# Self-attention values by token tiles, attention parts fetched three ahead and expert rows four ahead, and the last bias as a product with ones

## The chip, the cores and the metric

The kernel is one program on one core of one Trainium2 chip, written against the engines' own instructions, with a tile framework that allocates buffers and sets semaphores. The metric is the device time of one execution in microseconds (us), of which the median of several runs is taken. The core has TensorE (PE: matmuls and transposes; its weight loads are listed as PEld), VectorE (DVE), ScalarE (ACT), GpSimd (POOL) and SyncE (SP, which issues DMA transfers in order). In this kernel nearly all transfers are issued on SP.

## The reference

One decoder layer over 16 batches of 100 tokens, 512 wide, in float32: causal self attention, cross attention to 361 context tokens with grouped heads, and a mixture of 8 experts of which each token uses two. Every stage ends in a sum with its input and a layer norm.

```python
x = _layernorm(x + _L0_attn_ref(x, w_q, w_k, w_v, w_o))        # 16 heads of 32, causal
x = _layernorm(x + _L0_xattn_ref(x, ctx, mask, ...))           # 16 heads of 128, 4 kv heads, RMS-normed q, k
x = _layernorm(x + _L0_ffn_ref(x, ...))

def _L0_ffn_ref(x, ...):
    logits = x @ router_w + router_b;  topk_w = softmax(top2(logits))
    h = silu(x @ expert_w[e] + expert_b[e])                    # only the chosen two count
    combined = sum_e h_e * topk_w_e
    y = x + (combined @ proj_w + proj_b)
    return norm_w * (y / sqrt(mean(y*y) + 1e-6))
```

## The kernel before

All products are float32 products made from pairs. `split` (L133) makes of a float32 tile a rounded high half (a cast, mostly on ACT, L137) and a low half (a subtraction on DVE or POOL, L140); `mm3` (L143) is three matmuls, high by high, low by high and high by low (L145, L146, L147). In instruction names WH and WL are the halves of a weight or of a shared buffer. A product over 512 is four chunks of 128, so 12 matmuls. Most engines' work is emitted in Python order and then ordered by a scheduler; `in_turn` and `keep_in_program_order` pin single instructions. Each engine runs its own queue in order, and a buffer of a pool is taken anew when the last reader of its old tile is done.

The work is staged as follows.

- A, self attention (0 to about 215 us). Four groups of four batches (400 tokens), four chunks of four heads each: 16 units `heads4`. Extra work (splits, the next group's queries, keys and values, and the loads of stage B) is put between the steps of a unit by a table, `at(unit, step, function)` (L488 to L537). `self_v(g, r)` (L301) makes the values of one batch: 100 tokens as columns of the stationary side, 512 columns moving, 12 matmuls, and one copy from PSUM to the tile `v` by ACT.
- B, output product, residual, layer norm, cross-attention queries (to about 400 us).
- C, cross attention (about 400 to 1073 us). For each of 16 batches and 4 kv heads, one head group: `x_scores` (L736), softmax on DVE, ACT and POOL, transposes `x_turn` (L762), `x_attend` (L771), and the store of the result `o` to DRAM (`od`, L792). The loop L862 to L899 writes out the order by hand, with the next batch's key and value products between. In the last batch there is no next batch, and parts of stage D are put there instead.
- D, output product of cross attention, by parts: a part is one tile of 128 tokens (T of 13) times the four heads of one kv head (g of 4), 48 matmuls into a PSUM bank `acc`. The last three tiles are walked g by g. `d_load(i)` (L817) fetches the part's attention result `of` from DRAM on SP and splits it to `ot_h`, `ot_l`; `d_part(i)` (L826) is its product; `d_norm(t)` (L846) fetches the residual `x1d`, adds, normalises and stores to `x2d`; `d_turn(t)` (L928) transposes the tile for the router, and then adds the last bias, `x2+pb`, on POOL (L941) and stores that to DRAM as `xbd` (L942). `d_logits` (L944) is the router product. Routing (choose, settle and slots, L1058 to L1277) is a long chain of small DVE operations with a few products `gb`. `load_expert(e)` (L1337) loads and splits four rows of an expert's weights at once, at some tiles of the loop L1351 to L1387. In the pool `d_in` there are 2 buffers of `of`; a part is fetched when its predecessor's split has freed a buffer.
- E, expert slots: `e_gather` (L1296) fetches the tokens of a slot from `x2d` by index, then turn, product `ph`, bias `eb`, activation, store.
- F, the end: combine, and the last product. `f_load` loads the bias-carrying residual `z` from `xbd` (L1503 to L1507) and `x2`; `f_product` (L1536) is 12 matmuls into `pp`; `f_square` (L1543) adds `pp` to `z` (L1546) and squares.

## Time and profile before

| | |
|---|---|
| runs (3): median, lowest, highest | 1408.28, 1403.09, 1411.89 us |
| the profiled execution: its time | 1403.04 us |
| its span, first to last instruction | 1401.2 us |
| granted TensorE clock, mean | 0.979 |
| matrix instructions on PE | 7952 |
| DMA over the span | 159.79 MB, mean 114 GB/s |

The profile is one execution. Busy times are shares of its span; the slices divide the span in 40, a digit is the busy share of a slice in tenths. In rows of waits, "A <- B: total, times, longest" says that A's engine waited for B. In a timeline a row is start, duration, engine, line, operation, out<-in, shape, and in brackets the idle time of that engine before it and what ended it. Matmuls overlap: the time that one costs is the distance of its start to the next start, and not its duration.

### The profile page before, as it was taken

What the parts mean: (1) busy time and instruction counts of PE and PEld (TensorE: products, weight loads), DVE (VectorE), ACT (ScalarE), POOL (GpSimd) and SP (SyncE); (2) the same over time, 40 slices, a digit from 0 to 9 for tenths busy, and PEclk for the clock granted to TensorE, in tenths of its full rate; (3) what the DMA queues carried; (4) which work ended last, traced back from release to release, by engine and by line L of the source; (5) the groups of instructions that cost most, each with busy time, mean ns of one, the idle gap of its engine ahead of it and who ended that gap; (6) DMA issues with size and microseconds to landing.
All of it is one profiled execution on the core that took longest, in us unless ns stands there. A gap on an engine that the chain in (4) does not pass through costs nothing. (4 is left out here: it accounts for less than half of the span.)

```text
span 1401.2 us, 25131 instructions
## 1 busy us (share of the span) xinstructions
PE 1334.0 (95%) x7952; PEld 1107.1 (79%) x7952; DVE 938.7 (67%) x2932; ACT 757.9 (54%) x1899; POOL 712.5 (51%) x839
## 2 busy tenths in 40 slices
PE   8999989999999999999999999999999898899995
PEld 7888878888878888888888878888888676687783
DVE  5766576766556777777777666777754557764587
ACT  4666653444445666666666656666654233333356
POOL 6877763344245455555555545555554545532630
PEclk9999999999999999999999999999999999899997
DMA  5231144654452123323333123322435544667874
GB/s 160 73 94 49 58 143 127 141 105 116 90 108 60 50 69 75 72 71 78 77 70 75 46 64 78 77 65 55 108 107 155 197 165 151 188 228 254 271 239 152
DMA packets 197872, 159.79 MB, mean 114 GB/s; under 512 B 133322, under 2 KB 152878, under 8 KB 197742
## 3 DMA queue, kind: packets, MB, share of 16 engines
q1 hardware_dynamic: 187904, 137.83, 35.6%
q0 software_dynamic: 4576, 14.95, 3.5%
q10 hardware_dynamic: 5262, 5.41, 1.3%
q8 instruction: 65, 1.06, 0.3%
q14 instruction: 65, 0.53, 0.1%
HBM read 107.16 MB, written 50.99 MB: 113 GB/s over the span
## 5 line engine op out<-in xcount | busy, mean ns | idle before, releaser
L759 POOL TENSOR_SCALAR p<-p,sums 100x361 f32<-100x361 f32 x256 | 146.5, 577 | 100.0 <-DVE sums L758 89.0
L746 DVE CUSTOM_DVE_ANT_0 p<-s,nmask 100x361 f32<-100x361 f32 x256 | 132.9, 526 | 63.9 <-PE s L147 55.2
L757 ACT ACTIVATE p<-p,nm 100x361 f32<-100x361 f32 x256 | 153.2, 601 | 40.3 <-DVE nm L746 37.0
L140 DVE TENSOR_TENSOR pT_l<-ptp,pT_h 128x400 fp32r<-128x400 f32 (+1 forms) x192 | 107.4, 567 | 56.2 <-ACT pT_h L137 55.5
L145 PE MATMUL pq<-WH 128*128 128x512 f32 (+2 forms) x272 | 106.7, 392 | 6.2 <-DVE WH L139 5.4
L140 POOL TENSOR_TENSOR cT_l<-cf,cT_h 128x512 fp32r<-128x512 f32 (+1 forms) x48 | 54.3, 1133 | 104.6 <-ACT cT_h L137 102.6
L767 PE MATMUL ptp<-ident,p 100*128 100x100 f32 (+1 forms) x768 | 107.2, 251 | 0.0
L137 ACT CAST pT_h<-ptp 128x400 fp32r<-128x400 f32 (+1 forms) x192 | 91.2, 486 | 29.6 <-PE ptp L767 29.2
L767 PEld LDWEIGHTS ptp<-ident,p 100*128 100x128 f32 (+1 forms) x768 | 95.3, 151 | 13.3 <-POOL p L759 2.3
L146 PE MATMUL pq<-WL,WH 128*128 128x512 f32 (+2 forms) x272 | 104.0, 382 | 0.0
L147 PE MATMUL pq<-WH,WL 128*128 128x512 f32 (+2 forms) x272 | 103.8, 381 | 0.0
L147 PE MATMUL acc<-WH,ot_l 128*128 128x512 f32 (+1 forms) x208 | 85.9, 414 | 7.8 <-DVE ot_l L140 6.3
L145 PE MATMUL acc<-WH,ot_h 128*128 128x512 f32 (+1 forms) x208 | 85.5, 411 | 5.7 <-ACT ot_h L137 5.7
L145 PE MATMUL s<-kT_h,WH 128*100 128x362 f32 x256 | 87.7, 353 | 0.7 <-ACT kT_h L137 0.7
L145 PE MATMUL av<-pT_h,WH 128*128 128x400 f32 (+1 forms) x192 | 76.8, 400 | 8.7 <-ACT pT_h L137 8.3
L146 PE MATMUL acc<-WL,ot_h 128*128 128x512 f32 (+1 forms) x208 | 84.3, 405 | 0.0
L147 PE MATMUL s<-kT_h,WL 128*100 128x362 f32 x256 | 84.2, 329 | 0.0
L614 POOL TENSOR_TENSOR qs<-qs,r_q 128x512 f32<-128x512 f32 (+1 forms) x52 | 54.0, 1069 | 59.4 <-DVE r_q L169 49.3
L146 PE MATMUL s<-kT_l,WH 128*100 128x362 f32 x256 | 83.7, 327 | 0.0
L140 POOL TENSOR_TENSOR WL<-qf,WH 128x400 fp32r<-128x400 f32 x64 | 67.3, 1053 | 30.0 <-ACT WH L137 26.2
L145 PE MATMUL pv<-WH,cT_h 128*128 128x512 f32 (+1 forms) x192 | 79.9, 416 | 0.9 <-DVE WL L140 0.9
L146 PE MATMUL pv<-WL,cT_h 128*128 128x512 f32 (+1 forms) x192 | 78.1, 407 | 0.0
(337 smaller groups left out, 4003.5 us busy)
## 6 DMA issues: line engine op xcount, KB each, us to landing
qf<-qd SPq DMA_DIRECT2D x64, 200.0 KB, 2.9
of<-od SPq DMA_DIRECT2D x48, 256.0 KB, 3.6
cf<-in_ctxT SPq DMA_DIRECT2D x16, 722.0 KB, 4.1
eb<-in_expert_b SPq DMA_DIRECT2D x32, 256.0 KB, 4.3
ysd<-h SPq DMA_DIRECT2D x32, 256.0 KB, 4.4
f_e<-in_expert_w SPq DMA_DIRECT2D x30, 256.0 KB, 4.6
f_wq<-in_Wq SPq DMA_DIRECT2D x16, 256.0 KB, 3.3
f_wo<-in_Wo SPq DMA_DIRECT2D x16, 256.0 KB, 4.4
```

The costliest lines, as they stand in the source:

```text
L137: ins = nc.scalar.copy(dst.h, src)
L140: low.tensor_tensor(dst.l, src, dst.h.bitcast(FP), ALU.subtract)
L145: nc.tensor.matmul(out, a.h, b.h, start=start, stop=False)
L146: nc.tensor.matmul(out, a.h, b.l, start=False, stop=False)
L147: nc.tensor.matmul(out, a.l, b.h, start=False, stop=stop)
L614: nc.gpsimd.tensor_tensor(qr[:, hs, :], qr[:, hs, :], rs[:n, hs].unsqueeze(2).to_broadcast([n, GR, HD2]), ALU.mult,)
L746: nc.vector.tensor_tensor_reduce(out=p, in0=sc[:, :SE], in1=nmask, scale=1.0, scalar=BIG, op0=ALU.add, op1=ALU.min, accum_out=nm,)
L757: nc.scalar.activation(p, p, AF.Exp, bias=nm, scale=-1.0, accum_out=sh)
L759: nc.gpsimd.tensor_scalar(p, p, sh, 1.0, ALU.mult, ALU.mult)
L767: nc.tensor.transpose(pt[:n, h, :], probs[h][:, c0 : c0 + n], ident[:S, :S])
```

## The change

Three things change, and some buffers with them.

1. Values of self attention. Group 0 is made by batch as before (`self_v_batch`). For groups 1 to 3, `self_v(g, t)` makes three tiles of 128 tokens, and their rows are moved by SP from SBUF to SBUF into the four batches' tiles. The remaining 16 tokens of each of the three groups (48 in all) come through a new input `xlT` and one product `self_v_last`. Stage B's pools open and its loads start some steps later.
2. Inputs of D. The fetch of a part (`d_fetch`) is parted from its split (`d_load`). The first five parts are fetched into `d_in`, the later ones, three ahead, into the pool `xsp` (4 buffers, tag `xs`), which is also that of the gathered tokens and opens when C has closed. Expert weights are fetched row by row, four rows ahead, and one row is split every two parts, behind the part's own cast. Gathers are emitted at the fourth part from the end. Router weights load earlier.
3. The last bias. `x2+pb`, its 13 stores and 13 loads go. `pb` is split to two rows, 0 and 32, of a 33-row tile, and a matmul with ones adds it to `pp` in PSUM; `f_square` adds `x2` instead of `z`. Small tiles of the end share tags, and `z` has 4 buffers instead of 5.

```diff
@@ -298,15 +301,59 @@
-    def self_v(g, r):
-        pv = bank("mm" if g else "t", [S, D], f"pv_{g}_{r}")
+    def self_v_batch(r):
+        pv = bank("t", [S, D], f"pv_0_{r}")
         mmk(
             pv,
-            lambda k: xg[g][:, k, r * S : (r + 1) * S],
+            lambda k: xg[0][:, k, r * S : (r + 1) * S],
             lambda k: units["wv_s"][:, k, :],
         )
-        V[g, r] = w1.tile([S, D], FP, name=f"v_{g}_{r}", tag="v", bufs=8)
-        nc.scalar.copy(V[g, r], pv)
+        V[0, r] = w1.tile([128, D], FP, name=f"v_0_{r}", tag="v", bufs=8)
+        nc.scalar.copy(V[0, r][:S], pv)
+    NL = (NG - 1) * REST_V
+    def fetch_x_last():
+        XF["l"] = stage.tile([128, D], FP, name="xl_f", tag="f")
+        nc.sync.dma_start(XF["l"][:, : KC * NL], xlT.rearrange("p k n -> p (k n)"))
+    def split_x_last():
+        xg["l"] = slot_of(5)[:, 0, : KC * NL].rearrange("p (k n) -> p k n", n=NL)
+        f = XF["l"][:, : KC * NL].rearrange("p (k n) -> p k n", n=NL)
+        split(xg["l"], f, nc.vector, nc.gpsimd)
+    def self_v_last():
+        pv = bank("mm", [NL, D], "pv_last")
+        mmk(pv, lambda k: xg["l"][:, k, :], lambda k: units["wv_s"][:, k, :])
+        V["l"] = w4.tile([NL, D], FP, name="v_last")
+        nc.scalar.copy(V["l"], pv)
+    def self_v(g, t):
+        pv = bank("mm", [128, D], f"pv_{g}_{t}")
+        mmk(
+            pv,
+            lambda k: xg[g][:, k, t * 128 : (t + 1) * 128],
+            lambda k: units["wv_s"][:, k, :],
+        )
+        for r in range(GB) if t == 0 else ():
+            V[g, r] = w1.tile([128, D], FP, name=f"v_{g}_{r}", tag="v", bufs=8)
+        if t == 0:
+            vt = V[g, 0]
+        else:
+            vt = xp.tile([128, D], FP, name=f"vt_{g}_{t}", tag="f", bufs=2)
+        nc.scalar.copy(vt, pv)
+        a = S if t == 0 else t * 128
+        while a < (t + 1) * 128:
+            r, o = divmod(a, S)
+            m = min(S - o, (t + 1) * 128 - a)
+            nc.sync.dma_start(V[g, r][o : o + m], vt[a - t * 128 : a - t * 128 + m])
+            a += m
+        if t == 2:
+            a = (g - 1) * REST_V
+            nc.sync.dma_start(V[g, GB - 1][S - REST_V : S], V["l"][a : a + REST_V])
...
@@ -474,9 +521,9 @@
-    def fetch_row(name, s, src, k):
+    def fetch_row(name, s, src, k, p=stage):
         units[name] = slot_of(s)
-        f = stage.tile([128, D], FP, name=f"f_{name}_{k}", tag="f")
+        f = p.tile([128, D], FP, name=f"f_{name}_{k}", tag="f")
         tc.keep_in_program_order(nc.sync.dma_start(f, src[:, k]))
@@ -505,9 +552,14 @@
                     at(u, 1, split_x, g + 1, 2 + k)
-            if c > 1:
-                for r in range(2):
-                    at(u, 1 + 2 * r, self_v, g + 1, 2 * (c - 2) + r)
+            if c == 2:
+                at(u, 1, self_v, g + 1, 0)
+                at(u, 3, self_v, g + 1, 1)
+            if c == 3:
+                at(u, 1, self_v, g + 1, 2)
+    at(2, 1, fetch_x_last)
+    at(2, 3, split_x_last)
+    at(3, 0, self_v_last)
@@ -526,12 +578,12 @@
     AHEAD = 5
-    at(10, 0, b_open)
-    for t, i in enumerate((44, 48, 52, 54, 58)):
+    at(12, 0, b_open)
+    for t, i in enumerate((48, 50, 52, 54, 58)):
         at(i // 4, i % 4, b_fetch, t)
-        i += 2 if t == AHEAD - 1 else 4
+        i += 2 if t in (0, AHEAD - 1) else 4
         at(i // 4, i % 4, behind, b_split, t)
-    for t, i in enumerate((51, 55, 59, 61, 62)):
+    for t, i in enumerate((53, 56, 59, 61, 62)):
         at(i // 4, i % 4, b_out, t)
...
@@ -576,6 +628,10 @@
     nc.vector.tensor_scalar(nmask, nmask, -1.0, None, ALU.mult)
+    rw = kvk.tile([128, KC, NE], FP, name="rw")
+    nc.scalar.dma_start(rw, router_w.rearrange("(k p) e -> p k e", p=128))
+    rb = kvk.tile([128, NE], FP, name="rb")
+    nc.scalar.dma_start(rb, router_b.partition_broadcast(128))
     qkw = const.tile([128, 3], FP, name="qkw")
@@ -804,24 +860,33 @@
     order = [(b, g) for b in range(B) for g in range(NKV)]
-    OT, X1 = {}, {}
+    OT, OF, X1 = {}, {}, {}
+    split_last = [None]
         inp["d"] = pool(d_i, "d_in", 2)
+        inp["of"] = inp["d"], "f"
+    def d_fetch(i):
+        t, g = parts[i]
+        n = TT[t][1]
+        p, tag = inp["of"]
+        f = p.tile([128, D], FP, name=f"of_{t}_{g}", tag=tag)
+        OF[i] = f = f.rearrange("p (h n) -> p h n", n=128)[:, :, :n]
+        nc.sync.dma_start(f, od[t][:, g * GR : (g + 1) * GR, :n])
     def d_load(i):
         n = TT[t][1]
-        p = inp["d"]
-        of = p.tile([128, GR, 128], FP, name=f"of_{t}_{g}", tag="of")
-        nc.sync.dma_start(of[:, :, :n], od[t][:, g * GR : (g + 1) * GR, :n])
-        OT[t, g] = pair(p, [128, GR, 128], f"ot_{t}_{g}", tag="ot")
-        split(OT[t, g][:, :, :n], of[:, :, :n], low=nc.vector if i % 2 else nc.gpsimd)
+        OT[t, g] = pair(inp["d"], [128, GR, 128], f"ot_{t}_{g}", tag="ot")
+        split_last[0] = split(
+            OT[t, g][:, :, :n], OF.pop(i), low=nc.vector if i % 2 else nc.gpsimd
+        )
@@ -863,8 +928,10 @@
                 d_open()
+                d_fetch(0)
                 d_load(0)
             for j in range(HEAD * g, HEAD * (g + 1)):
+                d_fetch(j + 1)
                 d_load(j + 1)
@@ -905,6 +972,8 @@
     xsp = pool(fin, "k_x", 4, side="right")
+    inp["of"] = xsp, "xs"
     gs = ExitStack()
@@ -913,14 +982,6 @@
-    rw = gw.tile([128, KC, NE], FP, name="rw")
-    nc.scalar.dma_start(rw, router_w.rearrange("(k p) e -> p k e", p=128))
-    rb = gw.tile([128, NE], FP, name="rb")
-    nc.scalar.dma_start(rb, router_b.partition_broadcast(128))
-    pb = gw.tile([128, D], FP, name="pb")
-    nc.scalar.dma_start(pb, proj_b.partition_broadcast(128))
-    xbd = [dram.tile([128, D], FP, name=f"xbd_{t}") for t in range(NT)]
     lg = gw.tile([128, NT, NE], FP, name="lg")
@@ -938,8 +999,6 @@
         nc.scalar.copy(XT2[t][:, :, :n], pt[:, :, :n])
-        nc.gpsimd.tensor_tensor(x2[:n], x2[:n], pb[:n], ALU.add)
-        nc.sync.dma_start(xbd[t][:n], x2[:n])
@@ -1334,32 +1393,61 @@
-    def load_expert(e, last=False):
+    def load_last(e):
         for k in range(KC):
-            if last and k > 1:
-                f = raw[:, k - 2]
-            else:
-                f = stage.tile([128, D], FP, name=f"f_e_{e}_{k}", tag="f")
-                tc.keep_in_program_order(nc.sync.dma_start(f, kp(expert_w[e])[:, k]))
             split(
                 slot_of(e)[:, k],
-                f,
-                nc.vector if last and k == 1 else nc.scalar,
-                nc.vector if last and k else nc.gpsimd,
-            )
+                raw[:, k - 2] if k > 1 else ROW.pop((f"e_{e}", k)),
+                nc.vector if k == 1 else nc.scalar,
+                nc.vector if k else nc.gpsimd,
+            )
+    BY = (NT - TAIL) * NKV
+    erows = [(e, k) for e in early for k in range(KC)]
+    split_at = [HEAD * NKV + 2 + 2 * r for r in range(len(erows))]
+    assert split_at[-1] < BY + TAIL
+    for g in range(NKV - 1):
+        first = BY + TAIL * (g + 1)
+        erows += [(wo_slot[g], k) for k in range(KC)]
+        split_at += [first + min(k, TAIL - 1) for k in range(KC)]
+    erows += [(wo_slot[-1], k) for k in range(2)]
+    split_at += [len(parts)] * 2
+    rows_in, rows_out = [0], [0]
+    ROWS = 4
+    def e_rows(i):
+        while rows_out[0] < len(erows) and split_at[rows_out[0]] <= i:
+            e, k = erows[rows_out[0]]
+            in_turn(split_row(f"e_{e}", k), split_last[0])
+            rows_out[0] += 1
+            e_fetch()
+    def e_fetch():
+        while rows_in[0] < min(rows_out[0] + ROWS, len(erows)):
+            r = rows_in[0]
+            fetch_row(f"e_{erows[r][0]}", erows[r][0], kp(expert_w[erows[r][0]]),
+                      erows[r][1], inp["d"] if r % 5 > 2 else stage)
+            rows_in[0] += 1
+    begun = HEAD * NKV + 1
+    e_fetch()
     for i in range(HEAD * NKV, len(parts)):
         t, g = parts[i]
+        while begun < min(i + 4, len(parts)):
+            d_fetch(begun)
+            begun += 1
         if i + 1 < len(parts):
             d_load(i + 1)
+        e_rows(i)
         among = {}
                 among = d_logits(t - 1)
-            if g == 0 and t in (2, 4, 6, 8):
-                load_expert(early[t // 2 - 1])
         elif t > NT - TAIL and g == 0:
@@ -1371,8 +1459,6 @@
                 d_norm(t)
-        if t == NT - 1 and g < NKV - 1:
-            load_expert(wo_slot[g])
         if (t, g) == (CUT, 0):
@@ -1382,12 +1468,10 @@
             slots(0, EARLY, CUT)
-        if (t, g) == (NT - 1, 1):
+        if i == len(parts) - 4:
             for k in range(4):
                 e_gather(k)
-    d_i.close()
-    ck_l.close()
-    load_expert(wo_slot[3], True)
+    load_last(wo_slot[3])
     e_turn(0)
@@ -1405,6 +1489,8 @@
     d_l.close()
+    d_i.close()
+    ck_l.close()
     e_l = ExitStack()
@@ -1446,6 +1532,19 @@
+        f = stage.tile([128, D], FP, name="f_pb", tag="f")
+        b = inp["f1"].tile([33, D], FR, name="pb")
+        nc.gpsimd.memset(f[:33], 0.0)
+        for r in (0, 32):
+            nc.scalar.dma_start(f[r : r + 1], proj_b.rearrange("(o n) -> o n", o=1))
+        nc.scalar.copy(b, f[:33])
+        nc.vector.tensor_tensor(
+            b[32:33], f[32:33], b[32:33].bitcast(FP), ALU.subtract
+        )
+        inp["pb"] = b
+        inp["one"] = inp["f1"].tile([33, 128], FR, name="one_r")
+        nc.gpsimd.memset(inp["one"].bitcast(FP), 1.0)
     def f_weights(k):
@@ -1497,14 +1596,14 @@
         else:
-            z = inp["f2"].tile([128, D], FP, name=f"z_{t}", tag="z", bufs=5)
+            z = inp["f2"].tile([128, D], FP, name=f"z_{t}", tag="z", bufs=4)
             x2 = stage.tile([128, D], FP, name=f"x2_{t}", tag="f")
         L[t] = x2, z
-        for dst, src in ((z, xbd[t]), (x2, x2d[t0 : t0 + n])):
-            if not tail:
-                nc.sync.dma_start(dst[:n], src[:n])
-            else:
-                tc.keep_in_program_order(nc.scalar.dma_start(dst[:n], src[:n]))
+        src = x2d[t0 : t0 + n]
+        if not tail:
+            nc.sync.dma_start(x2[:n], src)
+        else:
+            tc.keep_in_program_order(nc.scalar.dma_start(x2[:n], src))
@@ -1537,18 +1636,22 @@
         pp = bank("av", [128, D], f"pp_{t}")
-        mmk(pp[:n], lambda f: cp[:, f, :n], lambda f: inp["pw"][:, f, :])
+        nc.tensor.matmul(
+            pp[:n], inp["one"][:, :n], inp["pb"], start=True, stop=False
+        )
+        for f in range(KC):
+            mm3(pp[:n], cp[:, f, :n], inp["pw"][:, f, :], False, f == KC - 1)
         F[t] = pp
         pp, (x2, y) = F[t], L[t]
-        nc.vector.tensor_tensor(y[:n], pp[:n], y[:n], ALU.add)
-        ss = tiny(1, f"yss_{t}", "yss")
+        nc.vector.tensor_tensor(y[:n], pp[:n], x2[:n], ALU.add)
+        ss = tiny(1, f"yss_{t}", "ln_v")
         nc.scalar.activation(pp[:n], y[:n], AF.Square, accum_out=ss[:n])
         to = C.pop(t) if t >= LATE else y
-        sn = tiny(1, f"yn_{t}", "yn")
+        sn = tiny(1, f"yn_{t}", "rs_y1")
         nc.vector.tensor_tensor_reduce(
...
```

More of the change, by code (lines that the diff above doesn't have):

```diff
@@ L31 @@
 GT = GB * S
+REST_V = GT % 128
 TT = [(t, min(128, T - t)) for t in range(0, T, 128)]
@@ L67, in tile_decoder_layer @@
     xT: bass.AP,
+    xlT: bass.AP,
     ctxT: bass.AP,
@@ L226, in tile_decoder_layer @@
     w3 = pool(a_l, "a_3", 8)
+    w4 = pool(a_l, "a_4", 1)
     ps.append(pool(a_l, "ps_a", 2, space=PSUM))
@@ L406, in self_attend @@
                     av[32 * j : 32 * j + 32, r, :],
-                    V[g, r][:, h : h + 32],
+                    V[g, r][:S, h : h + 32],
                     PT[g, c, j][:, r, :],
@@ L541, in tile_decoder_layer @@
     self_scores(*heads4[0])
-    self_v(0, 0)
+    self_v_batch(0)
     split_chunk(1)
     for r in range(1, GB):
-        self_v(0, r)
+        self_v_batch(r)
     self_q(0, 1)
@@ L1607, in f_first @@
         if t < REST:
-            s = tiny(1, f"s_{t}", "f_s")
+            s = tiny(1, f"s_{t}", "rs_a1")
             nc.vector.tensor_tensor(s, v, r, ALU.mult)
@@ L1612, in f_first @@
         nc.vector.scalar_tensor_tensor(y[:n], x2[:n], s[:n], y[:n], ALU.mult, ALU.add)
-        nm = tiny(1, f"nm3_{t}", "ln_nm")
+        nm = tiny(1, f"nm3_{t}", "rs_t1")
         nc.vector.tensor_scalar(nm[:n], F[t][1][:n], -(D**-1.5), None, ALU.mult)
-        var = tiny(1, f"var_{t}", "ln_var")
+        var = tiny(1, f"var_{t}", "rs_r1")
         nc.scalar.activation(
@@ L1791 @@
         "xT": x.reshape(NG, GT, KC, 128).transpose(0, 3, 2, 1),
+        "xlT": x.reshape(NG, GT, KC, 128)[1:, GT - REST_V :]
+        .transpose(3, 2, 0, 1)
+        .reshape(128, KC, (NG - 1) * REST_V),
         "ctxT": np.asarray(ctx_2048).reshape(B, SE, KC, 128).transpose(0, 3, 2, 1),
```

## The prediction

> **What bounds the kernel now.** I read the page's busy shares first, then its forty slices, then what TensorE (PE) waits for after 1050 us.
>
> ```profile
> span 1401.2 us, 25131 instructions
> PE 1334.0 (95%) x7952; PEld 1107.1 (79%) x7952; DVE 938.7 (67%) x2932; ACT 757.9 (54%) x1899; POOL 712.5 (51%) x839
> ...
> PE   8999989999999999999999999999999898899995
> ```
>
> PE is busy 95% of the span, so work taken off PE where its slices show 9 counts in full, and work taken off another engine counts only where PE waits for it. The dips are the first slice, slices 31 to 34 (the parts of the Wo product, stage D) and the end. The waits of PE from 1050 us on (us in total, times, longest) say who is late there:
>
> ```profile
> PE acc L147 <- DVE ot_l L140: 6.0, 5, 2.7
> PE acc L145 <- ACT ot_h L137: 5.7, 2, 2.9
> PE ptc L1526 <- DVE y L1517: 4.0, 2, 2.9
> ...
> PE acc L147 <- POOL ot_l L140: 1.5, 1, 1.5
> ```
>
> 13.5 us of D (6.0 + 5.7 + 1.5 and small ones, with 1.2 for `ptx` 14.7) go to halves of an attention part that are late. Who makes them late is in the waits of SP's queue, 1050 to 1250:
>
> ```profile
> SPq L851 <- DMA xbd<-x: 17.9, 8, 3.8
> SPq L822 <- POOL ot_l L140: 16.0, 10, 2.7
> SPq L942 <- POOL x L941: 11.6, 10, 2.6
> ```
>
> SP issues in order: the fetch of a part (L822) and the residual (L851) stand behind stores of `x2+pb`. One stall in the timeline, with ACT casting in order too:
>
> ```profile
> 1176.77 0.62 ACT L137 CAST WH<-f_e 128x512 fp32r<-128x512 f32 x1 [4.17 <-DMA f_e<-in_expert_w]
> 1177.30 0.40 ACT L137 CAST ot_h<-of 128x256 fp32r<-128x256 f32 x1
> ...
> 1177.75 0.45 PE L145 MATMUL acc<-WH,ot_h 128*64 128x512 f32 x1 [2.92 <-ACT ot_h L137]
> ...
> 1178.50 0.63 PE L145 MATMUL acc<-WH,ot_h 128*128 128x512 f32 x1
> 1178.93 0.63 PE L146 MATMUL acc<-WL,ot_h 128*128 128x512 f32 x1
> ```
>
> ACT sat 4.17 us on an expert row with the part's cast behind it. The matmuls after the gap start .43 us apart instead of .233: eight of them cost 8 × (.427 − .233) = 1.6 us more. That follows three gaps (near 1110, 1178 and 1192 us): 4.8 us on top.
>
> **The change part by part.** The sum goes against the profiled execution, 1403.04 us with a span of 1401.2. The three runs' median, 1408.28, lies 5.2 above it.
>
> *1. Self values by token tiles.* Groups 1 to 3 had 4 batches × 12 matmuls, 144; now 3 tiles × 3 × 12 = 108, and 12 for all the last rows (48): −24. The stream is 512 columns either way, and the trace has them .233 apart:
>
> ```profile
> 63.85 0.40 PE L145 MATMUL pv<-WH 128*100 128x512 f32 x1
> 64.08 0.39 PE L146 MATMUL pv<-WL,WH 128*100 128x512 f32 x1
> 64.31 0.39 PE L147 MATMUL pv<-WH,WL 128*100 128x512 f32 x1
> ```
>
> 24 × .233 = −5.6 us, in a stage where PE works 94 to 96% of the time, so it counts in full. Added: 18 SBUF row moves and one fetch on SP, a split on DVE and POOL; ACT copies 10 tiles for 12. A group's values are made one to two units ahead of use (16 units in 215 us: 13 us each); the nearest landings of transfers are 2.9 to 4.4 us, so the moves hide unless SP is held. The stage-B loads stand behind them and are themselves moved by up to 4 steps. Bounds −5.6 and +1; I take −5.6.
>
> *2. The end of cross attention (C).* This decides the sign. Parts from the sixth on are now fetched into the expert-gather pool, which opens after C closes and lies on C's memory. So the sixth fetch (`of` of tile 1, group 1) waits on SP for the last pT split and the last attend of C, behind two stores of the last `o` and a residual load. Before, C's last four head groups (1024 to 1073 us) were filled with acc matmuls of parts: 114 among 48 score, 56 transpose and 45 attend instructions. In the built order of the changed program there are none: 60 acc matmuls (five parts) stand before C's end instead of 203, so 143 (33.3 us at .233) move behind it. In the trace that stretch is full:
>
> ```profile
> 1020.00:1073.00 53.00, 52.70 (x285) 45.44 (x284) 24.63 (x69) 29.47 (x73) 26.18 (x30) 1.00 0.45 118
> ```
>
> (Columns: window, us, busy PE, PEld, DVE, ACT, POOL, granted clock, DMA share, GB/s.) Without filler PE has 48 × .165 + 56 × .075 + 45 × .182 = 20.3 us of starts there (start-to-start of score, transpose and attend in the same stretch), 5.1 a group. ACT has 4 × (.601 + .193) + 3 × .486 + .593 = 5.2 us a group (exponentials, a small scaling each, casts of pT, `o`) and DVE 4.75. Three engines that are equally full, with handoffs, do not run perfectly: I take 6.1 us a group, 4 us of idle PE (0 to 10). Then comes a hole after the last attend: scale `o` on ACT .59, three SP issues 1.2 (two stores .93, a residual .45 and the fetch .33 in the trace, partly together), the fetch 3.6 (2.4 to 6.3), a cast .62: 6.0, less about .6 of turns, 5.5 us idle (4 to 8), and 1.6 for the clock, probably. Sum +11.1 (+5 to +20).
>
> Who stands behind the waiting fetch on SP: the fetches of parts seven and eight, expert rows, the residuals `x<-x1d` and the x2d stores, all of stage D's input; for it waits ACT's cast, then DVE's or POOL's low half, then PE.
>
> *3. Stage D.* Gone: 13 `x<-x,pb` on POOL (median 1.29), 13 xbd stores on SP, expert rows as bursts of three. Parts are fetched three ahead (3 × 12 × .233 = 8.4 us against 3.6 landing); rows are split singly, two parts apart, four ahead. All of it is 13.5 + 4.8 = 18.3 us. But the last three stalls (2.92, .92 and 2.68, with two cold clocks 9.7 us) lie while DVE runs the routing:
>
> ```profile
> 1180.00:1190.00 10.00, 8.09 (x30) 5.32 (x29) 9.72 (x24) 4.13 (x7) 6.97 (x6) 0.91 0.46 155
> ```
>
> DVE is 97% busy; its chain from choose to slots takes 27 us (1171.5 to 1198.9), PE has 7 parts there, 84 × .233 = 19.6 us, in both orders. So at best about 2.4 of the 9.7 comes back. −(18.3 − 9.7) − 2.4 = −11.0 (−4 to −18.3).
>
> *4. Start of the experts.* Expert biases now load behind the stores of the last tiles, the first sum `h` on DVE stands behind the second product with the routing weights, and the second product waits for a bank that comes free later: +2.8, an estimate of four DVE passes of 512 columns (`x<-acc,x`, .69 each). Gathers come earlier, two activation-table loads (1.28 each, partly covered) and a POOL sum go: −1. I take +2 (−3 to +4).
>
> *5. Bias as a product.* 13 matmuls × .233 = 3.0; about six lie where PE is full (1.4), the rest beside ACT and DVE work at the end. The sum on DVE stays (`z<-pp,z`, .683 each). Six ACT issues of z (.33 to .5) and 13 stores and loads go. But the ones product takes its PSUM bank early and stands in PE's order before turns that must wait for a square. +1 (−3 to +5).
>
> Sum: −5.6 + 11.1 − 11.0 + 2 + 1 = −2.5. From the profiled execution 1400.5; from the median 1405.8: **1406 us**. One per cent, 14 us, is about what a measurement of this kernel can tell from no change.
>
> **The rivals.**
> *Faster.* The tail of C keeps pace (+5), and D gives back everything because DVE, rid of waits, works through the routing while PE still has parts (−18.3): −5.6 + 5 − 18.3 + 0 = −19, 1389 us. For it: PE's waits in D all name `ot` halves, not the routing. Against: DVE's 9.72 of 10.
> *Slower, by one mechanism: the tail of C runs cold.* Without filler PE waits in every group; if the gaps reach the 2.7 us that halved the clock in D, 20.3 us of starts become 20.3 × .427/.233 = 37 (+16.9), and with 10 us of waits and a 7 us hole C loses 34: −5.6 + 34 − 11 + 3 = +20, 1428 us. For it: softmax passes through DVE, ACT and POOL in turn, .53 + .60 + .58 for a head, before PE has its transpose. Against: scores of the next group are issued ahead, and four heads overlap. The change is slower at all once C loses over 13.6 us.
>
> Here a rule and the rows differ. In the rows above the granted clock fell after gaps of 2.7 to 2.9 us. The Trainium skill, "TensorE: Matmul & The Clock Gate" (Part 1), puts the fall after an idle window of about 3.4 us; gaps of 3 us in the tail of C would by that cost nothing but themselves, and this rival would be 1411 us, by the rows 1428. The rule also speaks against this change: it warns of every new idle gap over 3.4 us, and the hole behind C is one. It agrees with the 1.6 us that the rows put on it.
>
>
> *The values' gain does not show:* row moves queue behind weight loads on SP and PE waits for V, so term 1 becomes +1: sum +4, 1412 us.
>
> **How the numbers follow.** Forecast .45, the faster rival .28, the slower .19, the values' rival .08. The faster rival's spread crosses 1394 in some cases and the forecast's own range (1396 to 1416) hardly does: faster by over 1% .25, within 1% .58, slower .17. Range from the faster rival's time to just under the slower one's: 1388 to 1424; for the forecast alone 1396 to 1416.
>
> **What would show it.** Step 1: the last `pv` of self attention earlier, stage C starting about 5.6 us earlier. Step 2: no acc matmul after the fifth part until the last attend; PE busy about 20 of 24 us in the four groups, clock 1.00, then a hole of 5 to 6 us at `ot_h` of part six. Step 3: SP waits at the part fetch nearly gone, no POOL `x<-x,pb`, the first stalls gone, and PE waiting at the routing's `gb` near DVE's settle instead. Steps 4 and 5: slightly longer starts of `ph`, 13 products with ones. The forecast is wrong if PE is full in C's tail, if its clock drops there, or if PE meets no wait at the routing.

## The result, and the profile after

| | before | changed |
|---|---|---|
| median of the runs beside each other | 1408.17 us (4 runs) | 1426.05 us (4 runs) |
| ratio, 95% interval | | 1.0124 (1.0105 to 1.0142) |
| profiled execution: time, span | 1403.04, 1401.2 us | 1427.03, 1425.3 us |
| granted clock, mean | 0.979 | 0.967 |

The change costs 17.9 us. The forecast was 1406 us and the range ended at 1424. The runs below were made in five groups, each on one chip and beside the kernel before, which took medians of 1406.8 to 1422.6 us in them. So kernels are compared by their ratio to the kernel before in their own group; two kernels that were run in two groups each came out within .002 of themselves (1.0124 and 1.0107; 1.0065 and 1.0073). The profile of before lies at the low end of its runs: 1403.04 against 1408.

The head of the page of the changed kernel:

```profile
span 1425.3 us, 25092 instructions
...
PE 1343.6 (94%) x7941; PEld 1110.7 (78%) x7941; DVE 938.6 (66%) x2934; ACT 755.5 (53%) x1896; POOL 696.4 (49%) x829
...
PE   8999989999999999999999999999969997898985
```

PE has 11 instructions fewer, as counted, and is longer at work by 9.6 us, at a mean granted clock of .967 for .979. POOL lost 16 us of work. The slice with a 6 is new; a slice is 35.6 us, so it is the one from 1033 to 1068 us, with the hole at 1041 to 1053. What PE waits for from 1040 to 1220 us (total, times, longest):

```profile
PE acc L147 <- ACT ot_h L139: 10.1, 1, 10.1
PE acc L149 <- DVE ot_l L142: 8.9, 2, 5.5
PE pte L1363 <- ACT x2f L1001: 1.3, 1, 1.3
PE ph L147 <- DVE top L1125: 1.3, 1, 1.3
```

PE's many waits for halves of a part have become three: one of 10.1 us behind cross attention, and two (5.5 and 3.4) for low halves on DVE. These are the two causes that the experiments took apart. SP at the hole (start, duration, operation):

```profile
1039.68 1.39 SPq L527 DMA_DIRECT2D f_e<-in_expert_w  x3
1041.18 1.16 SPq L916 DMA_DIRECT2D x<-x1d  x2
1042.83 1.80 SPq L848 DMA_DIRECT2D od<-o  x2
1044.69 2.14 SPq L916 DMA_DIRECT2D x<-x1d  x1
1046.95 6.17 SPq L881 DMA_DIRECT2D of<-od  x4
```

and what SP waits for there (1038 to 1056 us):

```profile
SPq L881 <- DMA od<-o: 4.3, 1, 4.3
SPq L848 <- DMA od<-o: 1.5, 2, 1.0
```

The last attend is at 1040.6, and the fetch of the sixth part is issued 6.4 us later, behind expert rows, residuals and the last stores, with DMA at 93% of its time from 1041 to 1053 us. Its cast starts at 1052.57, 5.6 us after the issue. (The fetches behind it come later still: the 4.3 us are the seventh part's fetch, waiting for a store of the last `o` to land.) The matmul comes at 1053.24, and starts at half speed:

```profile
1053.24 0.79 PE L147 MATMUL acc<-WH,ot_h 128*128 128x512 f32 x1 [10.08 <-ACT ot_h L139]
1053.83 0.63 PE L148 MATMUL acc<-WL,ot_h 128*128 128x512 f32 x1
1054.26 0.63 PE L149 MATMUL acc<-WH,ot_l 128*128 128x512 f32 x1
...
1059.37 0.40 PE L149 MATMUL acc<-WH,ot_l 128*128 128x512 f32 x1
1059.61 0.39 PE L147 MATMUL acc<-WH,ot_h 128*128 128x512 f32 x1
```

Starts are .43 us apart until 1059.37: 14 matmuls in 6.1 us, where .233 each would be 3.3.

By landmarks of PE (the last matmul of each kind), in us:

| stage | before | changed | difference |
|---|---|---|---|
| A and B, to the last query product | 395.2 | 393.0 | −2.2 |
| C, to the last attend, with 143 matmuls (33.3 us) taken out of the changed one's D | 678.1 | 647.6 + 33.3 | +2.8 |
| D, to the last acc, without those 33.3 us | 134.4 | 139.4 | +5.0 |
| E, to the last expert product | 146.5 | 156.6 | +10.1 |
| F, to the end of the span | 47.0 | 55.4 | +8.4 |

The sum is +24.1, the difference of the spans. About 5 us of it is that the profile of before was a short execution: the run with the values alone, whose E and F are the same code, took 199.1 us for E and F where the profile of before took 193.5. The +2.8 of C is small beside what C differs by between executions: 678 us in this profile of before, 688 in a run below with the same order of matmuls there.

Stage E, before and then changed (window, us, busy PE, PEld, DVE, ACT, POOL, granted clock, DMA share, GB/s):

```profile
1207.70:1354.20 146.50, 136.72 (x698) 110.31 (x698) 88.91 (x246) 61.79 (x114) 56.68 (x58) 0.94 0.75 243
1213.30:1369.90 156.60, 143.33 (x697) 112.72 (x697) 86.50 (x246) 58.65 (x110) 54.26 (x57) 0.91 0.68 216
```

Of its 10.1 us, 3.5 are idle time of PE (13.3 for 9.8), and for 6.6 PE is longer busy with practically the same instructions, at a lower clock.

### The profile page after: what moved, and what is told of

It is laid out like the page before. It is cut to its first block, busy times and chain, and to the rows that moved or that the text cites. A ratio compares the mean times of both kernels' runs of the same rounds, so it can differ in the third digit from the quotient of the medians.

```text
span 1425.3 us, 25092 instructions
## 1 busy us (share of the span) xinstructions
PE 1343.6 (94%) x7941; PEld 1110.7 (78%) x7941; DVE 938.6 (66%) x2934; ACT 755.5 (53%) x1896; POOL 696.4 (49%) x829
## 4 chain that ended last, share of the span: by engine, by line
PE 75%; DVE 11%; DMA 5%; ACT 3%; issue 3%; POOL 1%; SPq 1%; ACTq 0%; DVEq 0%; POOLq 0%
PE pq L147 4%; PE pq L148 4%; PE pq L149 4%; PE pv L147 4%; PE pv L148 3%; PE pv L149 3%; PE ptp L823 3%; PE acc L147 3%; PE acc L149 3%; PE acc L148 3%; PE pk L147 3%; PE pk L149 3%; PE pk L148 3%; PE s L147 3%; PE s L148 3%
## 5 line engine op out<-in xcount | busy, mean ns | idle before, releaser
L815 POOL TENSOR_SCALAR p<-p,sums 100x361 f32<-100x361 f32 x256 | 146.5, 577 | 106.3 <-DVE sums L814 95.3
L147 PE MATMUL acc<-WH,ot_h 128*128 128x512 f32 (+1 forms) x208 | 85.6, 412 | 10.1 <-ACT ot_h L139 10.1
L139 ACT CAST ot_h<-of 128x512 fp32r<-128x512 f32 (+1 forms) x52 | 31.3, 602 | 99.7 <-PE acc L148 74.4
L670 POOL TENSOR_TENSOR qs<-qs,r_q 128x512 f32<-128x512 f32 (+1 forms) x52 | 54.0, 1068 | 60.4 <-DVE r_q L171 49.4
```

The lines of the kernel that those rows point to most:

```text
L139: ins = nc.scalar.copy(dst.h, src)
L147: nc.tensor.matmul(out, a.h, b.h, start=start, stop=False)
L670: nc.gpsimd.tensor_tensor(qr[:, hs, :], qr[:, hs, :], rs[:n, hs].unsqueeze(2).to_broadcast([n, GR, HD2]), ALU.mult,)
L815: nc.gpsimd.tensor_scalar(p, p, sh, 1.0, ALU.mult, ALU.mult)
```

## The experiments

**The three parts alone.** Each part of the change was put alone on the kernel before.

*Values by tiles alone* (group 1 to 3 by `self_v(g, t)`, the stage-B table moved):

```diff
-                for r in range(2):
-                    at(u, 1 + 2 * r, self_v, g + 1, 2 * (c - 2) + r)
+            if c == 2:
+                at(u, 1, self_v, g + 1, 0)
+                at(u, 3, self_v, g + 1, 1)
+            if c == 3:
+                at(u, 1, self_v, g + 1, 2)
```

> The kernel before with the change of the self values alone. Theory: in the changed kernel's trace the last of self attention ended only 2.2 us earlier, not 5.6, because PE waited 2.9 us once for attend's input and its clock fell after it; here too 1 to 4 us faster (1404 to 1407). Rival, that the values' part is a loss which the trace hides in later stages (row moves on SP delay the loads of stage B): 3 us or more slower. Rival, that the work counts in full: 5.6 us faster.

Measured: 0.9999 of the kernel before (0.9976 to 1.0022). PE reached the end of A 2.9 us earlier (202.8 for 205.7) and the end of B 1.9 us earlier, and that is within the noise of the whole. The changed kernel has the same wait of 2.9 us at attend. PE and ACT there:

```profile
202.41 1.42 PE L452 MATMUL av<-pT,v 100*32 100x100 f32 x32 [2.88 <-ACT y_ln L160]
```

```profile
200.84 0.62 ACT L139 CAST olp_h<-ol 128x512 fp32r<-128x512 f32 x1 [0.92 <-DMA ol<-o1d]
201.80 0.47 ACT L442 COPY pT<-pt 100x400 f32<-100x400 f32 x1
202.17 0.20 ACT L160 ACTIVATE y_ln<-a_ln 128x1 f32<-128x1 f32 x1
```

Attend starts right behind the copy `pT`, its input, which stood on ACT behind the cast of a stage-B load that had not landed. So 1.9 to 2.9 of the 5.6 us show in the profile, and in the time nothing that its interval (3 us to either side) could tell: the full gain of 5.6 us and a loss of more than 3.1 us are excluded, the theory's gain is not shown. That the moved stage-B loads made the wait is the likely reading; no run tests it.

*Inputs of stage D alone* (`d_fetch`, `e_fetch`, gathers, router weights; the bias on POOL as before):

```diff
+    inp["of"] = xsp, "xs"
-            if g == 0 and t in (2, 4, 6, 8):
-                load_expert(early[t // 2 - 1])
+        e_rows(i)
```

> The kernel before with the new inputs of stage D alone (fetch three ahead into the gather pool, expert rows singly, router weights early); values and last bias as before. Theory, that the hole behind cross attention (12 us without matmuls and 16 matmuls at the low clock) is the main loss and stage D's own gain about 10 us: 5 to 12 us slower (1413 to 1420). Rival, that the loss is made by the last bias: within 3 us of the kernel before.

Measured: 1.0068 (1.0047 to 1.0090), by the medians 10.8 us slower, as the theory had it.

*Bias as a product alone:*

```diff
-        nc.gpsimd.tensor_tensor(x2[:n], x2[:n], pb[:n], ALU.add)
-        nc.sync.dma_start(xbd[t][:n], x2[:n])
...
+        nc.tensor.matmul(
+            pp[:n], inp["one"][:, :n], inp["pb"], start=True, stop=False
+        )
```

> The kernel before with the last bias as a product with ones alone. Theory, that the product takes its bank early and holds PE until a square is done (3.7 us and a fall of the clock, with 3 us of added matmuls), against stores and sums saved in stage D: 0 to 6 us slower (1408 to 1414), all of it in the last 60 us. Rival, that the freed POOL and SP in stage D pay for it: 4 or more us faster. Rival, that the bias is the main loss: 12 us or more slower.

Measured: 0.9958 (0.9942 to 0.9973), 6 us faster: the first rival. Stage D takes 127.1 us for 134.4. What PE still waits for there and at the start of E (1074 to 1210 us):

```profile
PE acc L147 <- DVE ot_l L140: 6.5, 2, 3.7
PE acc L147 <- POOL ot_l L140: 3.3, 4, 1.8
PE pte L1299 <- ACT xsT_h L137: 1.7, 1, 1.7
PE acc L145 <- ACT ot_h L137: 1.2, 1, 1.2
```

So a large part (7 us) of what the prediction booked under the new fetches of D (POOL's sums and SP's stores that hold them up) is had by the bias part alone.

**Do they add?** Pairs of them, beside the changed kernel on one chip.

> The changed kernel once more, as the anchor for the other three on the same chip, which is not the one of every earlier run. All theories: 1.010 to 1.015 times the kernel before.

Measured: 1.0107 (1.0071 to 1.0142).

*Changed kernel without the bias part*, run twice:

> The changed kernel with the last bias as before: added on POOL, stored to and loaded from DRAM. By the single parts (values 0, parts 10.8, bias 6 faster) it would be 1417 to 1418. Theory: the bias gains in the kernel before only because it takes POOL and SP work out of stage D's waits, which the new parts take away too; with them it costs, so this is 1415 to 1420, 6 to 10 us below the changed kernel. Rival, that values and parts hinder each other: 1424 or more.

> The changed kernel with the last bias as before, beside the changed kernel on one chip. It was 1.0065 times the kernel before, and the parts alone 1.0068. Theory, that with the new parts the bias product costs what it gains without them: 5 to 9 us below the changed kernel. Rival, that the difference between chips made this up: within 3 us of the changed kernel.

Measured: 1.0065 (1.0041 to 1.0089) and, beside the changed kernel, 1.0073 (1.0045 to 1.0100). The medians there are 1427.1 and 1431.9, but the intervals overlap: the direction fits the theory (the product costs once the new fetches are there), the size is not settled.

*Changed kernel without the inputs part* (values and bias):

> The changed kernel with the inputs of stage D as before: values and bias alone. By the single runs 0.9999 and 0.9958 of the kernel before. Theory, that the inputs of stage D make all of the loss: .994 to .998 times the kernel before, and 20 us or more below the changed kernel. Rival, that values and bias lose something together: 1.000 or more.

Measured: 0.9934 (0.9911 to 0.9956), 24.8 us below the changed kernel beside it (1407.1 and 1431.9). So the inputs of D make the whole loss, and cost more beside the bias part (24.8 us) than alone (10.8 us). The profiles fit the reason that the gain that they would have in D has been had already: without the moved 33.3 us D takes 137.2 us with the inputs alone for 134.4 before, but 139.4 in the changed kernel for 123.2 in this run.

**The hole behind cross attention.** First the filler was put back: the parts' inputs in buffers of D's own pool.

```diff
-        inp["of"] = inp["d"], "f"
+        inp["of"] = inp["d"], "of"
-    inp["of"] = xsp, "xs"
-    ROWS = 4
+    ROWS = 3
-        while begun < min(i + 4, len(parts)):
+        while begun < min(i + 3, len(parts)):
```

> The changed kernel, but with the parts' inputs in two buffers of stage D's own pool, which opens before cross attention ends, and so two ahead instead of three; expert rows three ahead in the common staging buffers. In the built order 111 matmuls of parts stand again in the last four head groups of cross attention. Theory, that the hole behind cross attention costs 12 to 16 us: 1410 to 1415. Rival, that the loss lies in the expert stage and the end: stays above 1420.

Measured: 1.0060 (1.0037 to 1.0083), median 1416.9. In the profile C and D together take 811.1 us for the changed kernel's 820.3 and the 812.5 of before, but E takes 159.0 for 156.6 and 146.5. Half of the loss is elsewhere, behind D: between theory and rival.

Then both pools, the first sixteen parts in D's own and the later ones in the gather pool:

```diff
-        p, tag = inp["of"]
+        p, tag, k = inp["of"] if i < OWN else (xsp, "xs", 4)
```

> The changed kernel, with the first sixteen parts' inputs in two buffers of stage D's own pool (two ahead) and the later ones in the gather pool, three ahead; expert rows three ahead in the common buffers. In the built order 103 matmuls of parts stand again in the last four head groups. Theory, that the hole behind cross attention is most of the loss of the parts: 9 to 14 us below the changed kernel, that is no more than 1.004 times the kernel before. Rival, that the routing chain on DVE takes back whatever stage D gains: 5 us or less below the changed kernel.

Measured: 1.0075 (1.0054 to 1.0097), 5.5 us below the changed kernel beside it, with intervals that overlap: nearer to the rival's size, but not by the rival's way. The hole was still there, with another owner. ACT in this run:

```profile
1082.73 1.14 ACT L139 CAST WH<-f_e 128x512 fp32r<-128x512 f32 x2 [5.38 <-DMA f_e<-in_expert_w]
1084.61 0.62 ACT L139 CAST WH<-f_e 128x512 fp32r<-128x512 f32 x1 [0.74 <-DMA f_e<-in_expert_w]
1085.14 0.59 ACT L843 ACTIVATE o<-av,bvT 128x400 f32<-128x400 f32 x1
1089.47 0.62 ACT L139 CAST WH<-f_e 128x512 fp32r<-128x512 f32 x1 [3.75 <-DMA f_e<-in_expert_w]
1090.00 0.58 ACT L1001 COPY x2f<-ptx 128x512 f32<-128x512 f32 x1
```

The last attend was at 1080.4; the scaling of `o` that it releases stood on ACT behind casts of expert rows that were not there yet, and the router's copy `x2f`, for which PE waited 9.9 us, behind another. The next run fetched the rows later:

```diff
-    e_fetch()
     for i in range(HEAD * NKV, len(parts)):
...
+        if i == HEAD * NKV:
+            e_fetch()
```

> Sixteen parts' inputs in stage D's own pool, the later ones in the gather pool, as in the run hybrid (1.0075), and the expert rows first fetched behind the part after the eighth's fetch order, so that no expert row's cast stands on ACT ahead of cross attention's last o. In hybrid, ACT waited 5.4 us for an expert row with that o behind it, and PE 9.9 us. Theory: those 9.9 us and the fall of the clock go, 9 to 13 us below hybrid, 0.998 to 1.001 of the kernel before. Rival, that another transfer is late there: 1.004 or more.

Measured: 1.0081 (1.0051 to 1.0111): the theory fell. `o` now follows the attend at once (1074.1), but PE waits 7.2 us all the same, for a router copy on ACT that stands behind layer norms, which wait for DVE's residual sums and those for `x1d`, landed at 1075.8 and later. The wait moved twice, from the part to the expert row to the residual. In these stretches the DMA engines were 93% busy (hybrid, 1080 to 1091 us) and 86% (here, 1074 to 1081); that they are what is short there fits all three runs, but no run takes transfers away to show it.

*The changed kernel with the first four expert rows fetched behind the sixth to eighth part:*

```diff
+        ins = nc.sync.dma_start(f, src[:, k])
+        if p_after:
+            in_turn(ins, p_after)
...
-    e_fetch()
+        if i == HEAD * NKV:
+            e_fetch()
```

> The changed kernel, but the first four expert rows are fetched behind the fetches of the sixth to eighth part and not ahead of them (on SP they stood before those fetches, in a stretch with the DMA engines 93% busy). Theory, that the hole behind cross attention is 10 us and not 5.5 because the part's fetch lands behind a burst of other transfers: the wait for ot_h falls from 10 us to 5 to 7, 3 to 5 us below the changed kernel, 1.007 to 1.009 of the kernel before. Rival, that the landing is slow by itself (memory reuse, the stores before it): unchanged, 1.010 to 1.013.

Measured: 1.0046 (1.0027 to 1.0064) against 1.0107 and 1.0124. What PE waits for from 1040 to 1220 us in this run:

```profile
PE acc L149 <- DVE ot_l L142: 8.9, 2, 5.5
PE acc L147 <- ACT ot_h L139: 6.6, 1, 6.6
PE pte L1367 <- DMA xs<-x2d,idx: 1.6, 1, 1.6
```

The wait for `ot_h` is 6.6 us for 10.1, and the waits for DVE are untouched. Shown: some 3.5 us of the hole were expert rows ahead of the part. Its fetch is now issued 2.0 us after the last attend, not 6.4, but its landing is no faster: the cast starts 6.4 us after the issue, 5.6 in the changed kernel. So what is left of the hole is a slow landing, and to that extent the rival holds. The time is .0061 to .0078 lower, 9 to 11 us, more than the 3 to 5 expected and more than the wait: E and F are shorter too, 202.6 us for 212.0 in the profiles, and why is not shown.

**The routing on DVE.** The changed kernel with all low halves from the 39th part on made by POOL:

```diff
-            OT[t, g][:, :, :n], OF.pop(i), low=nc.vector if i % 2 else nc.gpsimd
+            OT[t, g][:, :, :n], OF.pop(i), low=nc.vector if i % 2 and i < 38 else nc.gpsimd
```

> The changed kernel with the low halves of the parts from the 39th on all made by POOL, none by DVE. Theory A, that those halves stand behind the routing chain on DVE and only their place is wrong: the two waits of 5.5 and 3.4 us and the two falls of the clock go, 6 to 12 us faster, 1414 to 1420. Theory B, that the routing chain itself is the bound: the waits move to its product gb, and the time stays within 3 us of 1426.

Measured: 1.0061 (1.0036 to 1.0086), in another group than the changed kernel, .0046 to .0063 below it or 6 to 9 us. What PE waits for, 1040 to 1220 us:

```profile
PE acc L147 <- ACT ot_h L139: 10.3, 1, 10.3
PE gb L1321 <- DVE is_in L1306: 8.5, 2, 7.7
PE gb L1156 <- DVE chosen L1147: 4.0, 1, 4.0
```

The 8.9 us at `ot_l` became 12.5 us at the routing's own products, so the chain itself is late, as theory B said; the chain then is through earlier and the start of E is shorter (39.9 us from the last acc to the last slot product, 46.9 in the changed kernel), which theory B did not say. The waits went theory B's way, the time theory A's.

The same move on the kernel before with the bias part and its product with ones last:

```diff
-        split(OT[t, g][:, :, :n], of[:, :, :n], low=nc.vector if i % 2 else nc.gpsimd)
+        split(OT[t, g][:, :, :n], of[:, :, :n], low=nc.vector if i % 2 and i < 38 else nc.gpsimd)
```

> The kernel before with the bias as a product, the product with ones last, and the low halves of the parts from the 39th on made by POOL; values and parts' inputs as before. The product alone gave 1400.8. Theory, that ones first cost 3 to 5 us at the end and the halves behind the routing chain 3 to 6 us: 1391 to 1396. Rival, that both waits only move: 1399 to 1402.

Measured: 1.0035 (1.0015 to 1.0054), a loss against the 0.9958 of the bias alone in another group: both theories missed. Stage D took 140.8 us for 127.1, with 5.9 and 4.6 us at the routing's products.

Why the chain is slow shows on DVE and POOL. DVE in the changed kernel, then POOL in the same microseconds:

```profile
1180.02 0.16 DVE L1193 SCALAR_TENSOR_TENSOR opens<-lo,rj 128x6 f16<-128x6 f32 x1
1180.09 4.50 DVE L1202 TENSOR_SCALAR named<-seq,lo,token 128x128 f16<-128x128 f32 x6
...
1185.17 0.41 DVE L142 TENSOR_TENSOR ot_l<-of,ot_h 128x256 fp32r<-128x256 f32 x1
```

```profile
1180.19 1.36 POOL L142 TENSOR_TENSOR ot_l<-of,ot_h 128x512 fp32r<-128x512 f32 x1 [1.21 <-ACT ot_h L139]
1181.51 2.48 POOL L142 TENSOR_TENSOR WL<-f_e,WH 128x512 fp32r<-128x512 f32 x2
```

Six small operations take 4.5 us, from 1180.09 to 1184.59, and POOL subtracts from 1180.19 to 1183.99. In the run without the inputs part they take 1.62 us with POOL idle beside them (1180.8 to 1183.7). The low half that PE waits for comes right behind. Of the 20 operations `named` in the changed kernel the median takes .34 us and the longest 1.30, which is the length of one of POOL's subtractions. So expert rows spread singly keep POOL at work beside the chain. The test takes POOL's rows away there (six of them; the parts' own low halves stay):

```diff
-            in_turn(split_row(f"e_{e}", k), split_last[0])
+            in_turn(split_row(f"e_{e}", k, nc.vector if 38 <= i < 48 else None), split_last[0])
```

> The changed kernel with the low halves of the expert rows split between the 39th and the 48th part made by DVE, not POOL. In the trace the routing's DVE operations of about 0.2 us take 1.2 to 1.3 us, as long as one POOL subtraction, wherever one runs beside them, and six of them 4.5 us instead of 1.6. Theory, that POOL's subtractions hold DVE's small operations: the routing chain is shorter although DVE has some 8 x .69 us more to do, PE's waits for ot_l fall by 2 us or more, the time by 2 to 6 us. Rival, that DVE is only full: its chain grows by 5 us, the kernel is 2 to 6 us slower than the changed one.

Measured: 1.0053 (1.0034 to 1.0071). DVE and the waits of PE (1045 to 1216 us):

```profile
1181.15 0.16 DVE L1193 SCALAR_TENSOR_TENSOR opens<-lo,rj 128x6 f16<-128x6 f32 x1
1181.23 1.62 DVE L1202 TENSOR_SCALAR named<-seq,lo,token 128x128 f16<-128x128 f32 x6
1182.77 0.41 DVE L142 TENSOR_TENSOR ot_l<-of,ot_h 128x256 fp32r<-128x256 f32 x1
```

```profile
PE acc L147 <- ACT ot_h L139: 9.7, 1, 9.7
PE pte L1363 <- DMA xs<-x2d,idx: 4.2, 2, 2.9
PE gb L1321 <- DVE is_in L1306: 2.9, 1, 2.9
PE acc L149 <- DVE ot_l L142: 1.4, 2, 0.9
```

DVE has more to do and is done sooner: 8.9 us of waits are 1.4, and 2.9 at the routing's product. No `named` takes more than .34 us. The theory held, and the gain (.0054 to .0071 of the time, 8 to 10 us, in another group) is larger than expected. The Trainium skill, "SBUF — State Buffer" (Who interferes with whom), gives a rule: DVE in a mode that uses two ports contends with POOL, and so does DVE with two inputs in SBUF beside a POOL operation that reads there; in the first case whoever issues first holds the shared pair of ports for its whole instruction and the other blocks. The trace agrees for the six `named` operations (1.62 us alone, 4.50 beside POOL); which of the rule's cases it is no run here tells.

**The product with ones last.** In the changed kernel, and in values and bias without the inputs part:

```diff
-        nc.tensor.matmul(
-            pp[:n], inp["one"][:, :n], inp["pb"], start=True, stop=False
-        )
         for f in range(KC):
-            mm3(pp[:n], cp[:, f, :n], inp["pw"][:, f, :], False, f == KC - 1)
+            mm3(pp[:n], cp[:, f, :n], inp["pw"][:, f, :], f == 0, False)
+        nc.tensor.matmul(
+            pp[:n], inp["one"][:, :n], inp["pb"], start=False, stop=True
+        )
```

> The changed kernel with the product with ones moved from the first to the last of each bias sum's 13 matmuls. Theory, that it holds PE at the end because it takes its bank early (3.7 us and a fall of the clock): 3 to 6 us below the changed kernel, 1420 to 1423, and no wait of pp at the square. Rival, that the matmuls after it only wait in its place: within 2 us of the changed kernel.

> Values by tiles and the bias as a product, with stage D's inputs as before and the product with ones last in each sum. With ones first this was 0.9934 of the kernel before, with 4.4 and 1.6 us of waits of pp for a square. Theory, that these waits go: 0.988 to 0.992. Rival, that the wait moves to the next turn or cast: 0.992 to 0.996.

Measured: 1.0064 (1.0041 to 1.0087) and 0.9961 (0.9940 to 0.9983), where ones first gave 1.0107 to 1.0124 and 0.9934, in other groups. One is lower, the other not. In the second, PE's waits from 1356 us on are these:

```profile
PE pp L147 <- ACT pp L1612: 4.3, 1, 4.3
PE pp L147 <- ACT cp_h L139: 0.7, 2, 0.5
```

The wait for the square's bank did not go; the next matmul has it. The place of the ones product does not settle anything: the rival holds for the second run, the first stays open.

**Both repairs together**, the diffs of the rows fetched later and of the rows' low halves on DVE:

> The changed kernel with both single repairs: the first expert rows fetched behind the sixth to eighth part (alone 1.0046 of the kernel before), and the rows' low halves beside the routing made by DVE (alone 1.0053); the changed kernel itself was 1.0107 and 1.0124. Theory, that the two costs lie in different stretches and add: 0.998 to 1.001. Rival, that the second takes over what the first gives back at the routing: 1.003 or more.

Measured: 0.9984 (0.9965 to 1.0002): the two add, as the theory said. With the rows fetched behind the parts and their low halves off POOL beside the routing, the changed kernel is level with the kernel before. D without the moved matmuls takes 126.7 us for 139.4 (37 short products of the routing now come behind it, in E); E still takes 155.7.

And values and bias alone, with the second repair:

```diff
-            load_expert(wo_slot[g])
+            load_expert(wo_slot[g], low=nc.vector)
```

> Values by tiles and bias as a product, stage D's inputs as before (that was 0.9934 and, with the product with ones last, 0.9961), and in the three late expert loads the low halves made by DVE, not POOL. Theory, that POOL's subtractions hold the routing's operations here too: 0.988 to 0.993. Rival, that here DVE has no room, with 12 x .69 us added: 0.996 or more.

Measured: 0.9963 (0.9943 to 0.9984), no lower than the 0.9934 and 0.9961 of the versions that it was made from: the rival, and no gain is shown for the second repair without the new fetches. Values and bias alone, with stage D's inputs as before, have the lowest ratio seen and are faster than both kernels; from the bias alone (0.9958, 0.9942 to 0.9973) their interval (0.9911 to 0.9956) does not part them.

## Why the prediction was wrong, point by point

Three terms of the sum failed: the hole behind C (7.1 us became 14.2), the start of the experts and the end together (+3 became some +13), and the values (−5.6 became −2.2). With D 1.8 us short of its gain and the tail of C 1.2 us better, −2.5 becomes +18.5, which is the 24.1 us between the profiles less the 5.6 by which that of before was lucky. For the hole the traces show where the time went; for the end of the kernel the cause is open.

- *Values* (−5.6): PE has the 24 matmuls less, but the stage ends 2 to 3 us earlier, since the last units wait at attend (2.9 us); in the whole, 0.9999. That PE's full slices make such work count in full was the wrong step. The rival that it would not show was right in size, wrong in mechanism: PE's wait there follows a copy on ACT, not a row move.
- *Tail of C* (4 us idle): right in size. From the last part's matmul to the last attend it took 26.5 us, where its instructions at the prediction's distances of starts make 22.3; by the same count the last 49.4 us of before lost 1.7. The time is lost in starts that are further apart, not in idle time: PE's records, which overlap, cover 9.76 of 10 us from 1020 on, at full clock. So the sign that the prediction set, PE busy some 20 of 24 us, did not come (23.1 of 24 from 1017 on). The rival of the cold tail, which gave nearly the right total (1428 for 1426), was wrong, and its total was luck.
- *Hole behind C* (5.5 us idle, 1.6 for the clock): the step that failed first. I put 1.8 us from the last attend to the fetch's issue (the scaling and three issues) and its median landing, 3.6 us, behind it. From the end of that attend to the issue it was 6.0 us, behind four expert rows, residuals and stores on SP that wait for stores before them, and the landing in that burst took 5.6. So two thirds of the excess came before the fetch was issued. PE was idle 10.1 + 1.2 us, and 14 slow matmuls, not 8, cost 2.9: 14.2 us, 7 more than in the sum.
- *Stage D* (−11.0): without the hole 125.2 us (139.4 − 14.2) for 134.4, −9.2. Right in size and in the reason that held it back: the routing on DVE, where I left 7.3 us standing with the clock's share and 8.9 us and two falls of the clock stood. But I took the chain's 27 us as fixed; POOL's rows beside it made it longer, and what the fetches gain in D is nearly all had by the bias part alone (127.1 us), and more than all by values and bias (123.2).
- *Start of the experts and the end* (+2 and +1): too small. E was 10.1 and F 8.4 us longer, some 13 us together when the luck of the profile of before is taken off. The ones product does hold PE for a bank (3.7 us), as said, and PE waits at the start of E for routing and copies (4.8 us in the first 22 us) and once for a gather's half (2.6). More of E's excess is clock than waiting: from 1230 to 1240 us the granted clock was .50 with no idle time over 1.3 us in the 20 us ahead of it, and eleven `ph` matmuls started .43 us apart. What of this is the fetches' doing was not taken apart: E is 152 to 159 us in the versions with the new fetches, but 148.0 with all late low halves on POOL, and 146 to 149 without them, but 157.1 with the expert loads' low halves on DVE. It seems to go with the division of work between DVE and POOL ahead of it; how, stays open.

## What to carry to other kernels

A fetch that is issued earlier helps only if its buffer is free earlier: look at whose memory the new buffer lies on, and at everything that stands on the same queue between that release and the fetch. Price a transfer right after a release by what is issued ahead of it and in flight with it, not by its median. And when an operation is spread out on POOL, look at which small DVE operations then run beside it.

## What the runs showed of the hardware

- Beside a POOL subtraction of 128x512 (1.3 us), small DVE operations of .2 us take 1.2 to 1.3 us; six of `named` 4.50 us for 1.62.
- After a gap of 10 us the half clock lasted 6.1 us of work (14 matmuls at .43), after gaps of 2.7 to 2.9 us 3.4 us (8 matmuls): the price of a gap in clock is not one number. And it fell to .50 at 1230 us with no gap over 1.3 us in the 20 us ahead of it, right behind short transposes and router products.
- With the DMA engines 93% busy, a fetch of 256 KB landed 5.6 us after its issue (median before: 3.6), and the issues of four fetches stretched over 6.2 us on SP, where one takes .33 us else; 4.3 of that was a wait for a store's landing.
